# A planner's durations are changed in a one-core stack of four layers

## The chip, the cores and the metric

The kernel runs on one core of one Trainium2 chip. The metric is the device time of one execution in microseconds (us), and of several runs the median. Shorter is better.

## What is computed

The input is eight sequences of 1024 rows of 256 numbers, in f32. Four layers are added to it one after the other, each of the layer-normed rows:

```
x = x + decoder_layer(layernorm(x))     # linear attention with running sums, then gelu(h W1) W2
x = x + relu(layernorm(x) w1) w2        # 256 -> 1024 -> 256
x = x + softmax(Q K' / 16) V            # one head of 256, over all 1024 rows
x = x + fp4(silu(g) * u) fp4(w_down)'   # g, u = fp4(layernorm(x)) fp4(w_gate)', fp4(w_up)'
```

The linear attention has 16 heads of 16. It takes running sums of sigmoid(q) and sigmoid(k) along the rows, divides by them, takes running sums again, and weights the values with what comes out. `fp4` rounds blocks of 16 numbers to a grid of eight magnitudes with a scale per block.

## The kernel before

A chunk is 128 rows, a flow (p) is four chunks, so there are 16 flows of 512 rows and 64 chunks. The work is written as generators, one per piece: `linear_group`, `linear_span` and `linear_chunk` for the linear attention of a flow, `dense` for both feed-forward layers of 1024 (weights streamed in tiles `w_ff`, results `hidden`), `norms_1` and `norms_2` behind them, `soft_chunk` for the softmax and the fp4 layer of a chunk, and a few that prepare weights. A generator yields what its next instructions need (`pe(...)`, `dve(...)`, `act(...)`, `dma(...)`: tiles, free banks, a free buffer, a condition) and issues them when it is resumed.

In what order the pieces run is decided by `Plan` while the program is being built. `Plan.run` (line 274) looks at every piece, asks `ready` (line 254) when its need would be met, and resumes the one with the smallest key (line 286): shortest wait of TensorE, then how far it is from ripe, then whether it is for TensorE, then whether it stays with 32-wide matmuls, then its due place. After each instruction `took` (line 158) writes down when it would end by the plan's own durations: `free` holds when each engine is free, `done` when a tile is written, `used` when it was last used, `by` which engine wrote it. Nothing of that is in the program; it decides only the order. `Queue.issue` (line 315, the line that every recorded instruction carries) ties each instruction to the one before it on its engine, so that the engines run the plan's order. If the chip is later than the plan, the engine whose turn it is waits.

The steps that the text below names by tile:

- In `linear_span`: sigmoid to q and k; a running sum and a product to `prod`; head sums of prod on TensorE (`prod,hsum`); a reciprocal and `flow`; `spread`, which writes a packed 128 x 128 tile to DRAM and reads it back repeated over the partitions (four transfers of 256 KB); again running sums and head sums; `e`, an exp; `front`, a matmul that sums over earlier rows; `div`, then `scale`; a transpose of scale (`ident,scale`), and scale's own `spread`.
- In `linear_chunk`: `v` (matmul `wv,n0T`, bias on VectorE); `qz`, a copy of q split by parity; scores (`qz,k`), masked to `sc`; the attention itself (`sc,v_pad`, `q,kv_sum`); `wo,xo`, and a layer norm to `h`.
- In `soft_chunk`: `n2T,wqk` and `n2T,qT` for scores, their maximum (`mx`, `nmax`), `prob` by exp on ScalarE with the row sum as an accumulator, transposes (`ident,prob`), `vt,probT`, layer norm and fp4 of `n`, transposes, `wgT,xqT` and `wuT,xqT`, silu and product to `hid`, fp4, transposes, `wdT,hqT`, and the output `y`.

Matmul results lie in eight banks (`BANKS`), named `bank`. ScalarE needs one of four tables for gelu, exp, sigmoid and silu (`SETS`); a load is put in front of an activation when the table changes. All DMAs leave SyncE's queue (SP), in the plan's order; the framework gives them eight semaphores in turn, and a DMA waits for the landing of the one that had its semaphore before. GpSimd takes some additions and the power in the layer norms (`ln_ve`, `ln_rstd`).

Of the kernel before, what the change touches and what calls it, by code (L numbers as in the profile page):

```python
# [62 lines left out]
class Plan:  # L63
# [12 lines left out]
    def __init__(self, tc, nc):  # L76
        self.tc, self.nc = tc, nc
        self.free = {}
        self.done = {}
        self.by = {}  # L80
        self.banks = []
        self.live = {}
        self.slots = {}
        self.kind = {}
        self.size = {k: v[0] for k, v in TILES.items()}
        self.spare = False
        self.used = {}
        self.held = set()
        self.kept = set()
        self.last = {}  # L90
        self.act_set = 0
        self.tiled = False
        self.ran = self.slow = 0.0
        self.parts = []
        for name in ("tensor", "vector", "scalar", "gpsimd", "sync"):
            setattr(self, name, Queue(self, name))
# [61 lines left out]
    def took(self, queue, op, args, kw):  # L158

        aps = [x for x in list(args) + list(kw.values()) if isinstance(x, bass.AP)]  # L160
        outs = [kw["out"] if "out" in kw else aps[0]]
        if kw.get("accum_out") is not None:
            outs.append(kw["accum_out"])
        size = 1
        for ap in aps:
            n = 1
            for d in ap.shape[1:]:
                n *= d
            size = max(size, n)
        after = 0.06  # L170
        if queue == "tensor":
            size = 1
            for d in outs[0].shape[1:]:
                size *= d
            cost = size * (0.84e-3 if op == "transpose" else 1.68e-3)
            tiled = op == "matmul" and (kw["lhsT"].shape[-1] <= 32 or kw["lhsT"].shape[0] <= 32)
            if tiled:
                cost *= 0.25
            if tiled != self.tiled:
                cost += 0.2  # L180
            self.tiled = tiled
            after = 0.2
        elif queue == "vector":
            each = {"reciprocal": 6.2e-3, "tensor_tensor_scan": 2.15e-3}.get(op, 1.05e-3)
            cost = 0.15 + each * size
            if op == "tensor_scalar" and outs[0].dtype == BF16:
                cost = 0.16 + 0.26e-3 * size
        elif queue == "scalar":
            cost = (0.16 if op == "copy" else 0.26) + 0.82e-3 * size
            for x in args:  # L190
                if not isinstance(x, bass.AP) and self.SETS.get(x, self.act_set) != self.act_set:
                    self.act_set = self.SETS[x]
                    cost += 1.3
        elif queue == "gpsimd":
            cost = 0.55 + 0.7e-3 * size
            if op in ("tensor_scalar", "iota"):
                cost = 0.22
            elif op == "memset":
                cost = 0.1 + 0.9e-3 * size
        else:  # L200
            cost = 0.4
        start = self.free.get(queue, 0.0)
        for ap in aps:
            name = ap.tensor.name
            if self.by.get(name) != queue:
                start = max(start, self.done.get(name, 0.0))
            if name not in self.done and name in self.held:
                start = max(start, self.used[name])
        if queue == "tensor":
            if start - self.ran > 2.0:  # L210
                self.slow = start + 2.1
            if start < self.slow:
                cost *= 2
            self.ran = start + cost
        end = start + cost
        if queue == "sync":
            n = 4e-6 / 250e-3
            for d in outs[0].shape:
                n *= d
            self.free["rings"] = max(self.free.get("rings", 0.0), end) + n  # L220
            after = self.free["rings"] - end + 1.8
        self.free[queue] = end
        for ap in outs:
            self.done[ap.tensor.name] = end + after
            self.by[ap.tensor.name] = queue
        for ap in aps:
            name = ap.tensor.name
            self.used[name] = max(self.used.get(name, 0.0), end + after)
            if queue != "tensor" and name not in self.kept:
                self.held.discard(name)  # L230
# [1397 lines left out]
```

## Time and profile before

| what | value |
|---|---|
| median of three runs | 2684.94 us (2684.01 to 2687.68) |
| profiled execution | 2683.53 us |
| its span | 2681.8 us |
| granted TensorE clock, mean over the span | 0.991 |
| ACT_TABLE_LOAD | 320 recorded, 1283 ns each |
| HBM read, written | 188.17 MB, 20.71 MB |
| DMA engines' busy share (queue 1) | 26.7% |

The profile is of one execution. PE is TensorE's matmul, PEld its weight load, DVE VectorE, ACT ScalarE, POOL GpSimd, SP SyncE's queue. In rows of stretches, each engine's busy time stands with its number of instructions in brackets. In rows of waits the three numbers are the total, how many, and the longest. In the timeline the first number is the start, the second the time from start to end of the row's instructions, and in square brackets stands the engine's idle time ahead of it with what ended it. An f32 matmul is recorded as two instructions, a transpose as one.

### The profile page before, as it was taken

Reading aid. Unit: us, or ns where it says so; the run is one execution under the profiler, and the core shown is the slowest. Engines: PE = TensorE matmul, PEld = TensorE weight load, DVE = VectorE, ACT = ScalarE, POOL = GpSimd, SP = SyncE. Lnnn points to the kernel's source line nnn. Section 1 sums busy time; section 2 is a strip of 40 time slices with the busy share of each in tenths; the row PEclk is TensorE's granted clock in tenths of the full one; section 3 lists DMA queues with packets and bytes.
Section 4 is the critical chain, followed back from the end, with each engine's and each line's share of the span. In section 5 each row is a group of like instructions: output and inputs, shape, how many; then the busy total and the mean of one; then the engine's idle time right before and its main releaser. Section 6 shows DMA issues by size and latency. Waiting matters only on the chain.

```text
span 2681.8 us, 45726 instructions
## 1 busy us (share of the span) xinstructions
PE 2600.9 (97%) x16687; PEld 2016.8 (75%) x16687; DVE 1971.2 (74%) x4514; ACT 1258.6 (47%) x2442; POOL 585.4 (22%) x1101
## 2 busy tenths in 40 slices
PE   6999999999999999999999999999999999999998
PEld 4777777787777777777777777777777777787765
DVE  8779787867768768586786858778586876856576
ACT  2443544445444453545536464363544546344343
POOL 1332322222212313123131212213122131212000
PEclk8999999999999999999999999999999999999999
DMA  3334231323223222232323223132231322322100
GB/s 87 101 106 144 85 101 58 107 66 87 73 64 107 75 77 72 77 101 62 97 66 94 81 72 107 52 90 79 68 108 58 97 64 73 91 66 82 41 12 12
DMA packets 286815, 211.89 MB, mean 79 GB/s; under 512 B 24704, under 2 KB 275072, under 8 KB 286592
## 3 DMA queue, kind: packets, MB, share of 16 engines
q1 hardware_dynamic: 286592, 208.97, 26.7%
q8 instruction: 133, 2.18, 0.3%
q14 instruction: 90, 0.74, 0.1%
HBM read 188.17 MB, written 20.71 MB: 78 GB/s over the span
## 4 chain that ended last, share of the span: by engine, by line
PE 72%; DVE 18%; DMA 4%; ACT 2%; issue 1%; POOL 1%; SPq 0%; DVEq 0%; ACTq 0%; POOLq 0%
PE bank L315 72%; DVE prod L315 3%; DVE hid L315 2%; DMA spread<-packed 2%; DVE n L315 2%; DVE ln_st L315 1%; DVE div L315 1%; DVE u L315 1%; DVE spread L315 1%; DVE x_amax L315 1%; DVE res L315 1%; ACT L315 1%; DVE e L315 1%; DVE mx L315 1%; DVE q L315 1%
## 5 line engine op out<-in xcount | busy, mean ns | idle before, releaser
L315 PE MATMUL bank<-half,w_ff 128*128 128x256 f32 x2048 | 532.5, 383 | 8.3 <-DMA w_ff<-in_L_ffn_w_dram 3.8
L315 PE MATMUL bank<-w_ff,hidden 128*128 128x256 f32 x2048 | 530.5, 383 | 0.0
L315 ACT ACT_TABLE_LOAD x320 | 410.6, 1283 | 81.2 <-PE bank L315 76.6
L315 PEld LDWEIGHTS bank<-half,w_ff 128*128 128x128 f32 x2048 | 380.2, 191 | 81.7 <-issue 23.9
L315 PEld LDWEIGHTS bank<-w_ff,hidden 128*128 128x128 f32 x2048 | 370.1, 191 | 83.9 <-issue 39.3
L315 POOL TENSOR_SCALAR ln_ve<-ln_mv 128x1 f32<-128x1 f32 x384 | 95.5, 249 | 1434.3 <-DVE ln_mv L315 1424.2
L315 ACT ACTIVATE hidden<-bank,c_L_ffn_b 128x256 f32<-128x256 f32 x256 | 121.0, 473 | 319.0 <-PE bank L315 318.8
L315 POOL TENSOR_TENSOR ln_rstd<-ln_ve,neghalf 128x1 f32<-128x1 f32 x384 | 240.8, 627 | 32.0
L315 PE MATMUL bank<-n2T,qT 128*128 128x512 f32 x512 | 241.6, 595 | 0.9 <-ACT qT L315 0.9
L315 PE MATMUL bank<-vt,probT 128*128 128x256 f32 x1024 | 233.5, 382 | 0.0
L315 PEld LDWEIGHTS bank<-vt,probT 128*128 128x128 f32 x1024 | 194.3, 191 | 29.9 <-issue 2.3
L315 ACT ACTIVATE hidden<-bank,c_L_attn_b 128x256 f32<-128x256 f32 x256 | 121.6, 475 | 171.0 <-PE bank L315 169.5
L315 PE MATMUL bank<-wdT,hqT 128*128 128x256 f32 x768 | 178.4, 383 | 1.9 <-ACT hqT L315 1.9
L315 PE MATMUL bank<-wgT,xqT 128*128 128x352 f32 x512 | 173.6, 462 | 1.1 <-ACT xqT L315 0.9
L315 PE MATMUL bank<-wuT,xqT 128*128 128x352 f32 x512 | 172.4, 459 | 0.0
L315 DVE TENSOR_TENSOR sc<-bank,triu 128x512 f32<-128x512 f32 x256 | 159.8, 681 | 13.8 <-PE bank L315 13.4
L315 PEld LDWEIGHTS bank<-wdT,hqT 128*128 128x128 f32 x768 | 145.4, 192 | 22.5 <-ACT hqT L315 2.8
L315 DVE TENSOR_TENSOR hid<-hid,bank 128x352 f32<-128x352 f32 x118 | 60.9, 516 | 131.5 <-PE bank L315 88.2
L315 PEld LDWEIGHTS bank<-n2T,qT 128*128 128x128 f32 x512 | 93.1, 190 | 72.1 <-issue 63.3
L315 PEld LDWEIGHTS bank<-wuT,xqT 128*128 128x128 f32 x512 | 97.4, 190 | 54.1
L315 PEld LDWEIGHTS bank<-wgT,xqT 128*128 128x128 f32 x512 | 93.4, 190 | 39.5 <-issue 6.0
L315 DVE TENSOR_REDUCE mx<-bank 128x1 f32<-128x512 f32 x128 | 86.7, 677 | 45.7 <-PE bank L315 45.2
(214 smaller groups left out, 4365.0 us busy)
## 6 DMA issues: line engine op xcount, KB each, us to landing
w_ff<-in_L_attn_W_dram SPq DMA_DIRECT2D x512, 128.0 KB
w_ff<-in_L_ffn_w_dram SPq DMA_DIRECT2D x512, 128.0 KB
spread<-packed SPq DMA_DIRECT2D x90, 256.0 KB
x<-in_L_attn_inputs_dram SPq DMA_DIRECT2D x64, 128.0 KB
xr<-in_L_attn_inputs_dram SPq DMA_DIRECT2D x64, 128.0 KB
rows<-res SPq DMA_DIRECT2D x64, 128.0 KB
out_dram<-y SPq DMA_DIRECT2D x64, 128.0 KB
rows<-rows SPq DMA_DIRECT2D x56, 128.0 KB
```

The lines of the kernel that those rows point to most:

```text
L315: ins = method(*args, **kw)
```

## The change

It touches `Plan.took` alone, and one list in `Plan.__init__`. No generator, tile, buffer count or due place is edited.

- TensorE: a column costs 0.853 and 1.687 ns, for 0.84 and 1.68.
- VectorE: the engine counts as free 0.08 us ahead of an instruction's end; an instruction that reads what VectorE itself wrote waits for `done`, 0.035 us after the end; `scalar_tensor_tensor` with a one-column operand costs 0.06 more.
- ScalarE: free 0.1 us ahead of the end; a table load of 1.3 us is added to when the engine is free, and so comes ahead of the instruction's waits, where it was part of the instruction's cost; an accumulator costs 0.15 more.
- VectorE, ScalarE, GpSimd: an instruction also waits until its output tile was last used.
- GpSimd: waits for its own results too, and for each operand 0.05 us longer.
- A result is seen 0.035 us after the end, for 0.06 (TensorE's stays 0.2).
- DMA: an issue waits until the eighth one before it has landed.

```diff
+        self.landed = [0.0] * 8
...
-        after = 0.06
+
+        overlap, after = 0.0, 0.035
...
-            cost = size * (0.84e-3 if op == "transpose" else 1.68e-3)
+            cost = size * (0.853e-3 if op == "transpose" else 1.687e-3)
...
+            elif op == "scalar_tensor_tensor" and any(ap.shape[-1] == 1 for ap in aps):
+                cost += 0.06
+            overlap = 0.08
...
                     self.act_set = self.SETS[x]
-                    cost += 1.3
+                    self.free[queue] = self.free.get(queue, 0.0) + 1.3
+            if kw.get("accum_out") is not None:
+                cost += 0.15
+            overlap = 0.1
...
         start = self.free.get(queue, 0.0)
+        if queue not in ("tensor", "sync"):
+            start = max([start] + [self.used.get(ap.tensor.name, 0.0) for ap in outs])
         for ap in aps:
             name = ap.tensor.name
-            if self.by.get(name) != queue:
-                start = max(start, self.done.get(name, 0.0))
+            if self.by.get(name) != queue or queue in ("vector", "gpsimd"):
+                start = max(start, self.done.get(name, 0.0) + (0.05 if queue == "gpsimd" else 0.0))
...
+        if queue == "sync":
+            start = max(start, self.landed.pop(0))
         end = start + cost
...
-        self.free[queue] = end
+            self.landed.append(end + after)
+        self.free[queue] = end - overlap
```

## The prediction

> **What bounds the kernel now.** I read the busy shares of the page first, then three stretches of the span, then who TensorE's matmuls wait for, then single places in the timeline.
>
> ```profile
> PE 2600.9 (97%) x16687; PEld 2016.8 (75%) x16687; DVE 1971.2 (74%) x4514; ACT 1258.6 (47%) x2442; POOL 585.4 (22%) x1101
> ```
>
> ```profile
> 0.00:400.00 400.00, 357.57 (x2621) 278.13 (x2625) 321.30 (x796) 167.29 (x375) 105.90 (x216) 0.95 0.37 105
> 400.00:2480.00 2080.00, 2059.09 (x13272) 1603.35 (x13264) 1522.33 (x3427) 1012.31 (x1910) 469.83 (x859) 1.00 0.27 80
> 2480.00:2682.00 202.00, 184.23 (x803) 135.33 (x802) 127.55 (x292) 79.05 (x159) 9.71 (x26) 0.98 0.07 23
> ```
>
> The columns are PE, PEld, DVE, ACT, POOL, clock, DMA. TensorE is the bound: idle 42 us in the first 400, 21 us in the 2080 of the middle, 18 us in the last 202. The change removes no instruction, so only these holes can move.
>
> A busy matmul counts its pipelined end too, so I measured the holes from starts. In the timeline of single matmuls two of 256 columns stand 216 ns apart, 0.843 ns a column; start to start less columns is the hole. Holes over 0.35 us: 34 of 43.8 us together in the first 400 us, 32 of 26.0 us in the middle, 17 of 17.0 us at the end. These 87 us are all that an order can win. In the middle there are also 213 changes between full and 32-wide matmuls, 0.145 us each (30.7 us for the 212 of ordinary size).
>
> ```profile
> PE bank L315 <- DVE prod L315: 12.3, 11, 4.3
> PE bank L315 <- DVE n L315: 11.2, 7, 7.4
> PE bank L315 <- ACT prob L315: 7.7, 9, 1.5
> PE bank L315 <- DVE scale L315: 7.5, 5, 2.6
> PE bank L315 <- DVE v L315: 6.5, 9, 1.1
> PE bank L315 <- DMA w_ff<-in_L_ffn_w_dram: 3.8, 2, 3.1
> ```
>
> Most holes are a transpose or head sum placed too few matmuls behind what feeds it, which is what the planner's durations decide. Two places to see it:
>
> ```profile
> 151.70 1.17 PE L315 MATMUL bank<-qz,k 32*128 32x256 f32 x16 [2.54 <-ACT qz L315]
> ```
>
> ```profile
> 651.30 1.28 ACT L315 ACT_TABLE_LOAD   x1 [0.32 <-PE bank L315]
> 652.59 0.47 ACT L315 ACTIVATE hidden<-bank,c_L_attn_b 128x256 f32<-128x256 f32 x1
> 653.08 1.28 ACT L315 ACT_TABLE_LOAD   x1
> 654.38 0.69 ACT L315 ACTIVATE prob<-bank,nmax 128x512 f32<-128x512 f32 x1
> ```
>
> In the first, the scores of chunk 4 waited for scale's way through DRAM. In the second, two table loads and a gelu stand between the softmax's maximum and its exp; the transposes of prob came 1.5 us late.
>
> **What the Trainium skill says.** "ScalarE: Activation LUTs", section "What ACT_TABLE_LOAD costs": a load takes about 1283 ns and back-to-back ACTIVATEs overlap by some 93 ns. The trace agrees: 1.28 us a load, and two qz of 501 ns each end within 0.91. It also gives 1380 ns of drain a switch; here the ACTIVATE starts 0.01 us after the load, so I charge none. "VectorE: DVE Perf Modes", section "The DRAIN you can't avoid", has the next instruction wait for an empty pipe unless it is not held. Here independent ones overlap and dependent ones don't:
>
> ```profile
> 1358.77 2.48 DVE L315 TENSOR_TENSOR sc<-bank,triu 128x512 f32<-128x512 f32 x4
> ```
>
> Four of 681 ns (row of sc) would be 2.72, so each overlaps by 0.08. Of a dependent pair, a scan begins at 31.46, lasts 0.69, and its copy starts at 32.19: 0.04 later. The new constants 0.08, 0.1 and 0.035 are thus the trace's.
>
> **The change part by part.** It edits only the planner; what it costs is in the order that comes out. I put the changed order against the old one and counted the matmul work between a producer and its consumer (columns at 0.843 ns, two passes, a transpose one, a switch 0.15): the lead. A hand-off is late when the lead is below the time that the trace shows it needs. Both orders have the same 9198 matmuls.
>
> - Overlap, the 0.035, the 0.06 and the 0.15 (VectorE, ScalarE). The chain from the sums (front) to scale took 4.2 to 5.6 us in the trace where it ran freely, and the old order gave it 4.3 of lead in five of the later flows. In the new one, 13 of 17 have 5.4 to 6.5. The holes before ident,scale at 249, 853, 1174 and 1818 us were 2.19, 0.93, 1.09, 1.26: 5.5 us. The first flow keeps 1.1 of lead and its 2.81. The second and third have 4.3 and 4.4, against 5.4 and 2.7 before: 1.2 us stay or come. Net -4.3.
> - Table loads in front of waits, and the accumulator's 0.15. Exp to transposes of prob: the tenth of smallest leads rises from 3.2 to 4.7 us. Holes there sum to 10.1 us; I leave 3. Net -7.1. The order has four loads more (325 for 321), 5.1 us of ScalarE, which is 47% busy: nothing, as long as no consumer is near (rival below).
> - Shared DMA semaphores. All 1533 transfers leave SP's queue round eight semaphores, and each waits for the one eight before. SP shows this as almost no waiting (1.6 us on a w_ff), so on the chip nothing changes; in the plan transfers land later and what reads them is set later. Scale to the first qz: second flow 6.6 to 9.6 us of lead, 9.2 were needed, so the hole of 2.70 goes; third flow 6.8 to 6.0 costs 0.8. Head sum to head sum: second flow 14.8 to 16.5, the delays having come to 3.5, so -1.7; third 20.4 to 18.4: +2.0. One w_raw load moves ahead of the spread loads in SP's queue, and the w_ff load behind it comes no sooner than now. Net -1.6.
> - Readers on GpSimd (0.05 us). Its 384 pow results feed VectorE; 0.05 shifts places within the same wait. Bounds -2 to +2; 0.
> - Second head sum to front: leads fall from 3.4 to 5.1 us to 3.2 to 3.4. The trace ran it at 3.5 without a hole; with VectorE busy 0 to 6 us over 13 flows. I take +1.5.
> - Full to 32-wide changes: 264 become 254, 10 x 0.145 = -1.5.
> - Banks that VectorE's v frees: holes of 0.5 to 1.3 us in front of ident,n and half,w_ff, some 8 us. The new order puts two v matmuls, then the four transposes, then six v, where the old had transposes first. Between 0 and -8: -3, the low half, because it is the same queue.
> - The end: the last v multiplication has 16.7 us of matmul work behind it for 16.0, and its own chain of dependent steps is longer. 0, bounds -4 and +4. Here an idle TensorE also loses clock ("TensorE: Matmul & The Clock Gate", section "What's actually happening", where idleness restores the half rate): twelve wdT passes at 2669 us took 4.54 against 2.86 at 2676.
>
> Sum: -4.3 - 7.1 - 1.6 + 1.5 - 1.5 - 3 = -16.0. A thousand positions move, and holes where there were none are to be expected; I take back 4, a quarter: -12. The profiled execution took 2683.5 (span 2681.8 and 1.7 around it): 2671.5. The median of the runs shown, 2684.9, is 1.4 above it: 2673.
>
> **The rivals.**
> - Larger gain (0.12). If the plan's leads are nearly always met, the v holes go whole (-5 more), nothing is given back (-4) and head sums lose another 4: 2660. For it: the new order settles into a pattern that repeats every two flows (leads of 6.0 and 6.5 in turn). Against it: the first 65 us are a chain of VectorE that hardly changes.
> - No difference (0.20). New holes take the place of the old ones; 2684. For it: VectorE is 74% busy and its queue delays are in no lead. "It does not do what it says" is part of this: if 0.05 us here and there only permutes equals. Against: smallest leads of the middle vanish (nine under 1 us, now none).
> - Slower by table loads (0.13). The plan now begins a load ahead of the waits, but in the new order 110 of 325 stand behind a separate wait instruction, as at 651.30, where the load begins when the bank is there. There the plan is 1.28 us too early, and hidden, prob, and hid are read by the next transposes. If 17 such loads meet a lead with no slack, 17 x 1.28 = 22 against the 12 gained: +10 on 2685, so 2694. It passes no change at ten. For it: leads of 1 to 2 us in the middle rise from 65 to 84. Against: exp's leads grew.
> - Slower at the start (0.10). The wait for w_ff at the second flow (3.1 us now) stays, and five more such come in SP's queue, 15.5 us, with some 4 of clock lost after them: 2692.
>
> **How the numbers follow.** 0.45 for 2673, own range 2665 to 2679; with the larger gain, faster 0.57; same 0.20; slower 0.23. Differences below 0.2%, 5.4 us, are about what a measurement of this kernel can't tell from none. From 2657 to 2694 about 0.8 lie inside: all holes of the middle gone and 2 us more is 2657.
>
> **What would show it.** TensorE's waits on prob under 4 us and on scale under 5, qz's 2.5 gone; idle in the middle under 15 us; the end the same within 4. Wrong, if waits on prob or hidden grow behind a table load, or if new waits of TensorE on n and v make up the sum.

## The result, and the profile after

The changed kernel takes 2729.51 us, the median of four runs (2726.89 to 2732.28); the kernel before, on the same chip, 2684.62. The ratio is 1.0174, its 95% interval 1.0162 to 1.0186: 45 us slower, where the forecast was 12 us faster and its range ended at 2694.

First the busy shares of the changed kernel's page, then its three stretches, the last one 49 us longer than before (PE, PEld, DVE, ACT, POOL, clock, DMA share, GB/s).

```profile
PE 2625.5 (96%) x16687; PEld 2031.6 (74%) x16687; DVE 1967.7 (72%) x4514; ACT 1267.5 (46%) x2446; POOL 581.8 (21%) x1101
```

```profile
0.00:400.00 400.00, 360.05 (x2700) 279.74 (x2701) 328.79 (x807) 166.14 (x374) 113.02 (x223) 0.94 0.36 105
400.00:2480.00 2080.00, 2039.30 (x13010) 1582.90 (x13009) 1488.21 (x3358) 1012.30 (x1888) 451.32 (x836) 0.99 0.27 78
2480.00:2731.00 251.00, 226.18 (x980) 168.92 (x978) 150.68 (x351) 89.05 (x184) 17.42 (x42) 0.96 0.10 29
```

TensorE has the same 16687 matmul records and is busy 24.6 us longer: the same matmuls at a lower clock (0.981 over the span, 0.991 before). To see where, I looked for matmuls whose starts lie more than 1.75 times their columns' time apart; these ran at half clock, and I added up what they took beyond full clock. Split into the first 400 us, the last 200 us of the span and what lies in between, the 48.7 us of span come to:

| us | before | after | planned_banks | old_packed_banks | before_both |
|---|---|---|---|---|---|
| TensorE idle, first 400 us | 42.4 | 40.0 | 40.9 | 35.3 | 35.9 |
| idle in between | 21.7 | 40.7 | 27.4 | 16.8 | 10.4 |
| idle, last 200 us | 16.8 | 24.4 | 24.4 | 24.4 | 16.8 |
| half clock, in between | 0.6 | 17.6 | 0.6 | 0.8 | 0.3 |
| half clock, end | 3.3 | 8.4 | 5.3 | 8.3 | 3.5 |
| span | 2681.8 | 2730.5 | 2694.7 | 2682.0 | 2659.5 |

(The last three columns are experiments below.) After less before: -2.4 + 19.0 + 7.6 + 17.0 + 5.1 = 46.3 of 48.7. Now whom TensorE waits for:

```profile
PE bank L328 <- DVE n L328: 19.4, 17, 8.3
PE bank L328 <- DMA w_ff<-in_L_attn_W_dram: 15.1, 6, 3.1
PE bank L328 <- issue: 13.6, 6, 2.3
...
PE bank L328 <- DVE q L328: 7.3, 1, 7.3
...
PE bank L328 <- DVE scale L328: 3.2, 2, 2.8
...
PE bank L328 <- ACT prob L328: 1.8, 2, 1.4
...
PE bank L328 <- DVE v L328: 1.5, 7, 0.2
```

What the forecast wanted gone is gone: prob 7.7 to 1.8, scale 7.5 to 3.2, v 6.5 to 1.5, qz's row is not there. Two rows are new, six waits each: w_ff and "issue". A third has grown, n from 11.2 to 19.4: waits of 0.8 us at six places in the middle and four more in the last 200 us. The new order repeats every two flows (some 330 us), and so does each fault in it. The first of the two new places, SP's queue and then TensorE:

```profile
1806.81 0.89 SPq L328 DMA_DIRECT2D w_ff<-in_L_attn_W_dram  x2
1808.33 1.17 SPq L328 DMA_DIRECT2D packed<-flow  x2
1811.72 2.49 SPq L328 DMA_DIRECT2D spread<-packed  x4
1814.31 2.03 SPq L328 DMA_DIRECT2D w_ff<-in_L_attn_W_dram  x4
```

```profile
1814.78 1.03 PE L328 MATMUL bank<-w_ff,hidden 128*128 128x256 f32 x4
1818.82 2.08 PE L328 MATMUL bank<-half,w_ff 128*128 128x256 f32 x4 [3.01 <-DMA w_ff<-in_L_attn_W_dram]
1820.68 4.75 PE L328 MATMUL bank<-wdT,hqT 128*128 128x256 f32 x12
```

SP writes packed, waits 2.2 us for it to land, issues 1 MB of spread, and only then the next w_ff. TensorE waits 3.01 us for that w_ff, and then runs at half clock: 2.08 us for what takes 1.03, 4.75 for what takes 2.75. The Trainium skill, "DMA: Bandwidth & Descriptors", section "Two DMAs through the same engine are not ordered", asks for just this wait: a transfer that reads what another wrote must be issued behind the first one's semaphore. The trace agrees, and puts 2.2 us on it.

The second place bears the label "issue", time for which the profile shows no cause:

```profile
1899.42 0.48 DVE L328 TENSOR_TENSOR kv<-bank,bdiag 128x128 f32<-128x128 f32 x2
...
1899.97 1.36 PEld L328 LDWEIGHTS bank<-half,w_ff 128*128 128x128 f32 x4 [2.63 <-issue]
1900.01 2.05 PE L328 MATMUL bank<-half,w_ff 128*128 128x256 f32 x4 [2.26 <-issue]
```

In the program this weight load waits for VectorE's second kv product, which ends at 1899.90, 0.07 us earlier: the result goes into the bank that kv reads. The planner had counted on another bank, free 0.36 us before TensorE got there; the pool of eight buffers, which picks by its own rule, gave the one that kv frees 2.2 us after TensorE got there. By the planner's own times 29 results of the changed order lie in a bank that is freed more than 0.3 us after TensorE comes to it, together 29 us (24 of them are four in a row at each of six places, so these delays overlap); of the order before nine, together 4.4.

And the end:

```profile
2712.76 1.35 PE L328 MATMUL bank<-wuT,xqT 128*128 128x352 f32 x4
2721.39 1.51 PE L328 MATMUL bank<-ident,q 128*128 128x128 f32 x6 [7.29 <-DVE q L328]
2723.15 4.17 PE L328 MATMUL bank<-wdT,hqT 128*128 128x256 f32 x12 [0.25 <-ACT hqT L328]
```

The last chunk's fp4 now stands alone, and its twelve wdT take 4.17 us at mostly half clock. Before, the last two chunks went together, one's gates in the other's wait:

```profile
2662.95 1.35 PE L315 MATMUL bank<-wgT,xqT 128*128 128x352 f32 x4
2664.14 1.35 PE L315 MATMUL bank<-wuT,xqT 128*128 128x352 f32 x4
2667.89 0.88 PE L315 MATMUL bank<-ident,hid 128*128 128x128 f32 x6 [2.41 <-DVE hid L315]
2669.23 4.54 PE L315 MATMUL bank<-wdT,hqT 128*128 128x256 f32 x12 [0.46 <-ACT hqT L315]
2674.37 0.85 PE L315 MATMUL bank<-ident,q 128*128 128x128 f32 x6 [0.60 <-DVE q L315]
```

### The profile page after: what moved, and what is told of

Its sections match the earlier page's. It is cut to its first block, busy times and chain, and to the rows that moved or that the text cites. A ratio compares the mean times of both kernels' runs of the same rounds, so it can differ in the third digit from the quotient of the medians.

```text
span 2730.5 us, 45739 instructions
## 1 busy us (share of the span) xinstructions
PE 2625.5 (96%) x16687; PEld 2031.6 (74%) x16687; DVE 1967.7 (72%) x4514; ACT 1267.5 (46%) x2446; POOL 581.8 (21%) x1101
## 5 line engine op out<-in xcount | busy, mean ns | idle before, releaser
L328 PE MATMUL bank<-half,w_ff 128*128 128x256 f32 x2048 | 541.8, 388 | 34.5 <-DMA w_ff<-in_L_attn_W_dram 15.1
L328 PE MATMUL bank<-w_ff,hidden 128*128 128x256 f32 x2048 | 536.0, 385 | 0.0
L328 POOL TENSOR_SCALAR ln_ve<-ln_mv 128x1 f32<-128x1 f32 x384 | 105.6, 275 | 1487.3 <-DVE ln_mv L328 1478.7
L328 PE MATMUL bank<-wdT,hqT 128*128 128x256 f32 x768 | 186.0, 394 | 0.8 <-ACT hqT L328 0.8
L328 PEld LDWEIGHTS bank<-wdT,hqT 128*128 128x128 f32 x768 | 152.3, 200 | 24.4 <-ACT hqT L328 1.4
L328 PE MATMUL bank<-ident,n 128*128 128x128 f32 x512 | 92.5, 279 | 20.9 <-DVE n L328 19.4
```

The costliest lines, as they stand in the source:

```text
L328: ins = method(*args, **kw)
```

## The experiments

My theory at first: the loss is two faults that repeat, w_ff behind spread on SP and the bank of kv. Rivals: the loss is in new waits on n and behind table loads, so that a hole that is filled is only met again at the next wait; or it is the end. All ratios are to the kernel before on the same chip, with a 95% interval.

**The part on DMA semaphores moves nothing.** Without `landed` the planner writes the same order, instruction for instruction on all five engines, in the changed kernel; added alone to the kernel before it changes nothing either.

**spread_later.** Only SP's order differs:

```diff
+            if self.name == "sync" and names[0].startswith("spread") and plan.loads < 2:
+                plan.later.append((self, op, args, kw, names))   # issued behind the next w_ff pair
+                plan.took(self.name, op, args, kw)
+                return None
```

> The changed kernel, 2729.5 us, with one difference on SP's queue alone: where no w_ff pair stands between packed and its spread, the spread transfers are issued behind the next pair. The order of the other four engines is the changed kernel's. Theory (two repeated holes are the loss; one is the w_ff load that stands behind packed, its landing and 1 MB of spread): the six holes of 3.0 to 3.3 us before half,w_ff at 828, 1156, 1488, 1819 and 2150 us and near 125 us go at the five later places, 16 us, and with them some 3 us of half clock behind each, 15 us: about 2698, between 2690 and 2706. Rival (new waits on n and v and table loads are the loss, and a hole that goes is only met again at the next wait): at least two thirds comes back elsewhere, 2718 or more. Rival (the end is the loss): 2722 or more.

Measured 2725.21 us, 1.0153 (1.0138 to 1.0168), 4 us less. The holes before half,w_ff went, and TensorE's waits on n grew from 19.4 to 34.7 us: two of 1.5 where one of 3.0 had been. So the rival was right here; the time alone would have fitted the rival of the end too. Why, VectorE's queue shows:

```profile
1811.13 0.48 DVE L341 SCALAR_TENSOR_TENSOR res<-u,ln_rstd,xr 128x256 f32<-128x256 f32 x1
1813.74 0.69 DVE L341 TENSOR_TENSOR spread<-k,spread 128x512 f32<-128x512 f32 x1 [2.12 <-DMA spread<-packed]
```

VectorE waits 2.12 us for spread, and n stands behind that. By these rows the w_ff load and n are late by the same cause, the landing of packed; mending one uncovers the other.

**planned_banks.** The five orders are the changed kernel's; each result lies in the bank that the planner reckons with:

```diff
-        bank = ps.tile([P, 512], F32, tag="bank", name="bank")
+        k = plan.place()
+        bank = ps.tile([P, 512], F32, tag=f"bank{k}", name="bank", bufs=1)
```

> The changed kernel with the same order on all five engines; only, each matmul result lies in the bank that the planner reckoned with, where the pool of eight picks by its own rule. Theory: the hole of 2.26 us that the profile puts down to issue (578, 908, 1238, 1569, 1900, 2229 us) is a bank that VectorE's kv product has still to read, where the planner counted on one that was free 2.2 us earlier. Six holes of 2.4 us go, 14.5, and some 1 us of half clock behind each: about 2710, between 2704 and 2716. Rival (the time is in waits on n and v and in table loads): 2722 or more. Rival (these holes are a matter of instruction supply): no change, 2729.

Measured 2699.35 us, 1.0071 (1.0048 to 1.0094), with four runs between 2696 and 2709: 30.2 us less than the changed kernel, more than the 20 expected. The row "issue" is gone, and kv has taken its place with next to nothing:

```profile
PE bank L335 <- DVE n L335: 20.2, 17, 8.3
PE bank L335 <- DMA w_ff<-in_L_attn_W_dram: 16.3, 6, 3.6
...
PE bank L335 <- DVE kv L335: 2.2, 6, 0.4
```

The table has the 30: idle in between 40.7 to 27.4, half clock 17.6 to 0.6 there. The holes before half,w_ff stayed, and yet TensorE keeps its clock behind them:

```profile
1472.67 1.13 PE L335 MATMUL bank<-half,w_ff 128*128 128x256 f32 x4 [3.62 <-DMA w_ff<-in_L_attn_W_dram]
1473.64 2.75 PE L335 MATMUL bank<-wdT,hqT 128*128 128x256 f32 x12
```

**both_undone.** Both edits.

> The two edits together: spread behind the next w_ff pair, and the planner's banks. Theory: the two losses add up, 31 and 20 us: 2679, between 2670 and 2688, and then the forecast's own gain shows as what lies below 2684.6. Rivals: 2710 or more (time is met again at the next wait), or 2715 or more (the end).

Measured 2699.07 us, 1.006 (1.0045 to 1.0075): no better than planned_banks. The two do not add, as spread_later said; for SP's half my theory was wrong. The cause had to be taken away there, not its place moved.

**old_packed_banks and before_old_packed.** The landing itself is taken out of the way: spread reads another tile, so all later flows work with the first flow's weights.

```diff
+        early.append(flat)
+        src = early[0]
...
-                    tensor=flat.tensor,
-                    offset=flat.offset + 8 * b * 2 * GT,
+                    tensor=src.tensor,
+                    offset=src.offset + 8 * b * 2 * GT,
```

> planned_banks (2699.4 us) with one difference: spread reads the packed tile that the first flow wrote, not the one just written, so SP need not wait for packed's landing; the weights of all later flows are thus the first flow's, and the output is not the reference's. Orders are the changed kernel's. Theory (the planner issues spread 0.8 us behind packed where SP waits 2.8 us for the landing; w_ff loads and VectorE's product with spread, with n behind it, are both late by that): the holes before half,w_ff (16.3 us in all) shrink below 5 and the waits on n stay near 20, not 34 as in spread_later; with the half clock behind them 2672, between 2663 and 2682. Rival (the place is met again at whatever comes next): 2692 or more. Rival (it is the 1 MB of spread data ahead of w_ff, not the wait): holes before half,w_ff stay over 10 us, 2692 or more.

> The kernel before (2684.3 us) with the same difference: spread reads the first flow's packed tile, and the output is not the reference's. Theory: SP's wait for the landing is there too, but in this order it reaches TensorE at few places (w_ff 3.8 us, qz 2.5): 2678, between 2672 and 2683. Rival (the wait costs as much in every order, and is no part of what the change brought): 2665 or less.

Measured 2681.37 us, 0.9986 (0.9978 to 0.9993), and 2664.82 us, 0.9926 (0.9910 to 0.9941). So the landing costs the changed order 18 us and the order before 20: the rival of the second expectation was right. It is a cost that both kernels have, and no part of the 45. In the changed order w_ff's waits of 16.3 fell to 5.5, not quite the 5 expected (the 1 MB of spread still stands ahead of it), and n stayed at 19.3.

**before_planned_banks and before_both.** The same two in the kernel before.

> The kernel before with its order, and each result in the bank that the planner reckoned with. By the planner's own times nine results go into a bank freed 0.3 to 0.8 us later than it counts, 4.4 us together, where the changed kernel has 29 with 27 us. Theory: 2681, between 2676 and 2684. Rival (placing banks so is worth its 30 us in any order): 2665 or less.

> The kernel before with both differences (planned banks, and spread reading the first flow's packed tile, so that the output is not the reference's), to be set against old_packed_banks, 2681.4 us. Theory (bank and landing are separate costs): 2685 less 4 and 20, 2661, between 2656 and 2667; the changed order is then still 20 us behind with both costs out of the way. Rival (they overlap): 2668 or more.

Measured 2680.99 us, 0.9987 (0.9979 to 0.9996), and 2662.23 us, 0.9918 (0.9896 to 0.9939), both as expected. The banks are worth 4 us there and 30 in the changed order; that difference, 26 us, is most of the loss. With both costs out the changed order is 19 us behind, and the table has it: 6.4 idle in between, 7.6 idle at the end, 5.3 half clock. The new waits on n in the middle, six of 0.8 us, are still there, so they come from neither cost. What before_both does to the waits is the most telling view of the study. TensorE's rows in it:

```profile
PE bank L322 <- DVE prod L322: 7.8, 5, 4.3
PE bank L322 <- ACT prob L322: 7.7, 9, 1.5
PE bank L322 <- DVE scale L322: 4.9, 3, 2.6
...
PE bank L322 <- DVE v L322: 0.8, 2, 0.4
```

With not one duration changed, prod fell from 12.3, scale from 7.5 and v from 6.5: 26.3 to 13.5 together. Of the waits that the forecast wanted to shorten most, prob alone stayed, at 7.7.

**Parts left out.** Each is another order. no_accumulator stands on the changed kernel, the other three on planned_banks. In their turn:

```diff
-            if kw.get("accum_out") is not None:
-                cost += 0.15
...
-                    self.free[queue] = self.free.get(queue, 0.0) + 1.3
+                    cost += 1.3
...
-        overlap, after = 0.0, 0.035
+        overlap, after = 0.0, 0.06
...
-            overlap = 0.08
+            overlap = 0.0
...
-            overlap = 0.1
+            overlap = 0.0
...
-            if self.by.get(name) != queue or queue in ("vector", "gpsimd"):
+            if self.by.get(name) != queue:
...
-        if queue not in ("tensor", "sync"):
-            start = max([start] + [self.used.get(ap.tensor.name, 0.0) for ap in outs])
```

> The change without one of its parts, the 0.15 us for an accumulator on ScalarE; the order that comes out is another one throughout. In it a w_ff pair stands between packed and spread in every flow from the third on but one scale, and from 400 us on no result is put into a bank that is freed more than 0.3 us later than the planner counts. Theory (the loss is these two places, not the durations): no repeated hole, 2670, between 2660 and 2682. Rival (the durations themselves set new waits on n, v and behind table loads): 2700 or more. Rival (this part was what mattered for prob): waits on prob come back to 7 us or more, 2684 or more.

> planned_banks (2699.4 us) with the table loads counted in the activation's cost as before, which gives another order. If the placing of table loads is what brought the exps forward (waits on prob 1.5 us in planned_banks, 7.7 before), waits on prob come back to 5 us or more. Time: the forecast's term is 7 us, so 2706 if nothing else moved; but the order decides whether the late spread meets TensorE, so 2675 to 2710. If waits on prob stay under 3, the gain there came from another part.

> planned_banks without the overlap and dependence of VectorE and ScalarE (results 0.06 late, no wait for own results, no early start), another order. The forecast put the scale chain's 4.3 us on this part: then TensorE's waits on scale come back from 3.0 to 6 us or more. Time between 2695 and 2725, for the planner's own end is 38 us later. If the waits on scale stay under 4, the gain there was another part's.

> planned_banks without the part that lets an instruction wait until its output tile was last used, which the forecast did not price; another order. In it every flow's packed has a w_ff pair before its spread from the second on, and half of scale's have none. If the part matters by itself: 2710 or more, with new waits on hidden, prob or n. If it only draws another order: between 2675 and 2700, with waits on w_ff below 8 us.

| run | us | ratio | waits on prob, scale (us) | idle in between, last 200 us (us) |
|---|---|---|---|---|
| no_accumulator | 2685.67 | 1.0002 (0.9993 to 1.0011) | 9.5, 14.4 | 29.1, 22.1 |
| tables_as_before | 2679.33 | 0.9977 (0.9967 to 0.9986) | 7.8, 2.8 | 22.1, 16.1 |
| overlap_as_before | 2692.88 | 1.0032 (1.0022 to 1.0043) | 5.9, 9.8 | 19.1, 24.0 |
| outputs_unwaited | 2686.22 | 1.0008 (0.9999 to 1.0016) | 12.3, 2.8 | 28.8, 19.2 |

Against planned_banks (2699.35; 1.5 and 3.0) prob comes back without the table part and scale without the overlap, as the forecast had it. That does not single these parts out: prob comes back in all four, most of all without the wait for outputs, on which the forecast had put nothing, and scale most without the accumulator's 0.15. All four are faster all the same; overlap_as_before is even below the 2695 at which its range began. no_accumulator missed its 2670: it has neither fault, and six waits on scale and five on prob in their place, one per repetition. One duration less, then, and the order no longer meets kv's bank: that the changed order meets it six times is chance as far as the durations go. tables_as_before ends with 16.1 us idle, like the kernel before (16.8), and the other three with 19.2 or more. The runs below agree (16.8 with the durations of before, 21.5 to 24.3 with the changed ones): the table part goes with the costly end.

**The planner told of the landing.** landing_told lets SP wait in the plan for its own results; the other three only reckon a spread tile 2.3 us later. All have planned banks.

```diff
-            if self.by.get(name) != queue or queue in ("vector", "gpsimd"):
+            if self.by.get(name) != queue or queue in ("vector", "gpsimd", "sync"):
...
             after = self.free["rings"] - end + 1.8
+            if outs[0].tensor.name.startswith("spread"):
+                after += 2.3
```

> planned_banks with one more thing in the planner: SP also waits for its own results, so that spread is reckoned behind packed's landing. The order is another one; a w_ff pair or two stands between packed and spread at nearly every place. Theory (the landing is what the planner does not know): the waits on w_ff of the middle go, and VectorE's waits on spread fall; the chip falls 10 to 25 us behind the planner in the middle where it fell 40 in planned_banks. The planner itself now ends 46 us later, so the time is 2690 to 2715. Rival (the planner can hide the landing once it knows it): 2675 or less.

> The changed kernel with two corrections of what the planner believes: results lie in the banks it reckons with (as planned_banks), and a spread tile is reckoned to be there 2.3 us later, the wait that VectorE shows. Another order. Theory (with the two errors out, the change's durations are right and bring the gain that was forecast): the chip falls behind the planner by some 30 us in all, as before_planned_banks (30) and tables_as_before (28) did, on a planned end of 2632: 2663, between 2655 and 2674, and waits on prob under 4 us. Rival (the changed durations draw orders that lose 20 us by themselves, as old_packed_banks against before_both): 2680 or more.

> The kernel before with the same two corrections; the durations of before. Another order. Theory: it ends 15 to 35 us behind spread_late_banks, 2680 to 2695, since its planned end is 2661 and it keeps waits on prob of 6 us or more. Rival (all the gain is in the two corrections, none in the durations): within 8 us of spread_late_banks or below it.

> spread_late_banks without the wait for an output tile's last use; another order, with a w_ff pair between packed and spread in every flow. Theory: planned end 2638 and some 30 us: 2668, between 2658 and 2680. If that wait matters by itself, waits on prob or hidden of over 8 us and 2685 or more.

landing_told took 2703.45 us, 1.0069 (1.0050 to 1.0087). VectorE's waits on spread fell from 14.5 to 0.4 us, and the middle is the emptiest of holes of all complete kernels, while the first flows pay:

```profile
0.00:400.00 400.00, 346.23 (x2463) 266.89 (x2463) 319.24 (x770) 167.60 (x364) 106.25 (x208) 0.93 0.36 99
400.00:2500.00 2100.00, 2087.49 (x13477) 1628.20 (x13477) 1531.84 (x3465) 1007.69 (x1924) 472.79 (x872) 1.00 0.27 80
```

12.5 us idle in 2100, but 53.8 in the first 400. spread_late_banks took 2678.51 us, 0.9982 (0.9975 to 0.9989), before_late_banks 2681.81, 0.9992 (0.9982 to 1.0003), late_unwaited 2696.08, 1.0051 (1.0031 to 1.0071). The theory failed twice: spread_late_banks was to reach 2663 with little waiting on prob, and has 8.3 us of that, 0.9 us in each of six repetitions (before_late_banks has 14.5); and it leads before_late_banks, which has the durations of before, by 3.3 us only, where 15 or more were expected. The rival, that the gain is in the corrections, was right. late_unwaited, with the same corrections, is 14 us behind the kernel with durations of before, and has the long waits on prob (9.4) that were to show that the wait for a tile's last use matters by itself. But leaving that wait out had gained 13 us on planned_banks, and loses 18 here: a part has no price of its own, only one in each order. spread_late_banks and tables_as_before, 0.2% below the kernel before, are the fastest complete kernels found.

## Why the prediction was wrong

- **Table loads, -7.1, and scale, -4.3**: right as waits in this order (prob 7.7 to 1.8, scale 7.5 to 3.2). Not shown is that these parts did it: prob comes back whichever part is left out, and is 8.3 with every part in spread_late_banks.
- **Banks that v frees, -3**: v went from 6.5 to 1.5, but this is where the forecast failed. It counted leads from producer to consumer and took the banks for a side effect of VectorE's queue, with bounds of 0 and -8. A result also needs a place, and which bank it gets is not the planner's to say. No gain-only bound was justified: that step, on kv instead of v, cost 30 us in the new order, some 9 of them half clock behind the holes of w_ff (last section).
- **Taken back for new holes, 4**: mis-sized. Idle in between grew by 19 us and half clock by 17. Of the sign that I had named, new waits on n and v, half came: n grew by 8.2 us, v shrank by 5.0. I had seen that the order repeats every two flows and put it down in favour of a gain. It is what multiplies: one fault of 2.3 us is six.
- **Shared DMA semaphores, -1.6**: rightly without effect on the chip, but the moved leads that I put on it can't be its, for it moves nothing. The waits on w_ff that I gave a rival (five more of 3.1 us, 15.5) came in number and size, 18.3 us for 4.0; not at the start but throughout, and the kernel before has the same cost elsewhere.
- **The end, 0 with bounds of 4**: 7.6 us idle and 5.1 of half clock, 13. I had weighed the last v and not the last chunk's own chain of dependent steps with nothing beside it.
- **Clock**: the sum has no term for it; 22 of the 48.7 us are half clock.
- **87 us of holes are what an order can win**: the count was right and the reading of it wrong. I took waits on v, scale and prod for leads set too short by the durations. Half of those waits, and half of the 21.7 us of idle time in between, are the landing of packed and the pool's banks (before_both), which no duration in the change touches. What durations could win was mainly prob, some 6 us; with the planner's other two errors mended, the change is worth 3.3 us in the orders that came out.

So the mechanism of the loss is shown for banks (30 against 4 us) and, by the profile, for the end (13). That the landing costs 18 to 20 us is shown for both kernels, which takes it out of the difference. What decides on the half clock in the middle is read from the traces (last section). Open is why the changed durations draw the costly end; by tables_as_before it is the table part or an order drawn with it.

## What to carry to other kernels

A plan's error is worth what its order makes of it: before correcting durations, set the plan beside the trace and look where the lag jumps, for there is what the plan doesn't know, here a landing and a bank. Where the order repeats, count a new fault with its repetitions and the clock behind it. And a stall that is moved shows only its place: take away its cause, and do so in both kernels, before it is given a share of a difference.

## What was not expected of the hardware

The half clock does not follow from a hole's length here. In the changed kernel 8 of the 11 holes of 2.4 to 3.3 us between 400 and 2480 us were followed by half clock, 15.3 us in all; in planned_banks none of five of 3.0 to 3.8 us. The Trainium skill, "TensorE: Matmul & The Clock Gate", section "What's actually happening", says that activity is judged in windows of 3413 ns that run freely, so that it matters where in a window a hole falls. The traces agree: in all 17 of them each stretch of half clock that ends within the span lasts a whole number of steps of 3.413 us (1, 2, 3, 6 or 7).

So I laid this grid over every trace from 400 to 2480 us and measured how long TensorE was idle in each step at full clock. All 16 steps with 1.98 us or more were followed by a step at half clock; of some 10300 with less, two were (1.80 and 1.93 us). Two steps of the changed kernel around the hole at 1900 us, and three of planned_banks around the hole that ends at 1472.67 (TensorE busy, clock, DMA share, GB/s):

```profile
1896.43:1899.84 3.41, 1.31 (x7) 1.00 0.56 184
1899.84:1903.25 3.41, 3.24 (x8) 0.50 0.03 10
```

```profile
1467.59:1471.00 3.41, 1.47 (x6) 1.00 1.01 246
1471.00:1474.42 3.42, 1.75 (x8) 1.00 0.79 203
1474.42:1477.83 3.41, 3.41 (x20) 1.00 0.00 0
```

The hole of 2.3 us lies almost whole in one step, leaves it 2.1 us idle and costs the next one half its clock. The hole of 3.6 us is cut by an edge of the grid into 1.9 and 1.7 us and costs nothing. The orders repeat every 331 us in the changed kernel and every 324.3 in planned_banks, 97.0 and 95.0 steps: a hole comes back at nearly the same place in a step, so that one lucky or unlucky place counts four or five times. This is the 9 us by which planned_banks gained more than its six holes and the half clock behind those, and it is luck: `took` in both kernels reckons with half clock after any idle time of over 2.0 us, wherever it falls, and knows no grid. At the kernel's end the limit is less clean: a step with 1.6 us idle was followed by half clock in the kernel before and in the changed one.
